# Attention statistics and their first rows issued from ScalarE's queue, and computed earlier

## The chip, the cores and the metric

The program runs on one core of one Trainium2 chip. The metric is the device time of one execution in microseconds (us). A core has a matrix engine (PE, TensorE), a vector engine (DVE), a scalar engine (ACT, ScalarE), a general one (POOL, GpSimd) and a synchronisation engine (SP), each with an instruction stream of its own that it works off in order. In this program DMA transfers are issued from SP's stream, apart from a few at the start which are issued from ACT's.

## The reference

Eight images of 768 channels and 32 x 32 positions (1024 tokens), in fp32, pass two layers; each adds to its input what it computes from the group-normalised input.

```python
# layer 0: attention in which scores are an outer product of variances
q, k, v = qkv of gn(x), 12 heads of 64 channels
var_v = var(v, over the head's channels); var_k = var(k, likewise)
attn = softmax(var_v @ var_k.T * 64**-0.5); x = x + proj(attn @ v) + b
# layer 1: 1x1 convolution over the features and 28 local correlations
f = gn(x); fn = f / max(norm(f), 1e-12)
corr = [sum(shift(fn, r, c) * fn) for 28 offsets (r, c) of a 7 x 7 window]
x = x + conv1x1(concat(f, corr)) + b
```

The queries are not used. A score is a product of one number per query token (the variance of its value vector) and one per key token, so an exponential is computed by ScalarE from a row of `var_v`, broadcast over 128 partitions, with a scale per partition from `var_k`.

## The kernel before

Channels or tokens lie on the 128 partitions. Large products are made by a scheme with seven block products in place of eight (`PAIR`, `SINGLE`); product p = 1 comes first in its PSUM bank, and 6, 7 and 4 are added to the same bank after the vector engine has read what stood there (`Banks`, line 316; `BANK`, line 59).

**The stages of an image b.** `KeysValues` (line 506) multiplies the normalised image with the key and value weights in two halves of six heads (`half` 0 and 1), one unit of `KV_US` = 1.94 us after another, and takes head statistics of the results on DVE (`kbn`, `vbn`). After the last unit of a half, `spread` (line 601) makes variances of them on DVE (`head_m2`), and a maximum over the partitions on POOL (`most`). `values` turns the value variances with a PE transpose (`ptv`), copies them on DVE (`rsv`) and stores them in DRAM as rows (`vdr`): this is `to_rows`, line 498. `keys` makes `nk`, the scales of the exponentials, on DVE; `rows` stores them the same way (`ptk`, `rsk`, `kdr`), only where a pair of that half needs them.

`Attention` (line 826) works on six pairs of heads (`Pair`, hp = 0 to 5; 0 to 2 belong to half 0, 3 to 5 to half 1). Per pair, `Pair.rows` (line 660) loads for each head the row of `vdr` broadcast over 128 partitions (`bc`, 512 KB). Eight steps t follow. A step is two exponentials on ACT (`ex`, 128 x 1024, line 674) and eight products on PE (`av`, line 699); at most three steps of exponentials stand ahead of PE (`AHEAD`). PE runs four steps at a time (`STEPS`). The softmax denominators come in one of two ways. For pairs in `SUMMED` (3, 4, 5; in image 0 also 0) DVE adds the exponentials (`acc`), and PE sums over partitions. For the others ACT makes a second set of exponentials over rows of `kdr` (`bk`, also 512 KB) and keeps only their sums (`junk`, line 684). The inverse sums go through DRAM (`it`, `ir`, `di`) and come back broadcast (`rd`, line 771), and DVE multiplies them into the pair's result (`v<-v,rd`).

Then `project` (line 1185) makes the output projection, adds it to the image (`f`), stores it (`x1d`) and normalises it. `Corr` (line 997) makes products of f with itself (`gr`) and from them the correlations (`win`, `dd`, `dn`, the transpose `ct`, `cs`), and `Conv` (line 1090) the convolution of layer 1, in units of the class `Wide` (line 914), loading `x1d` back as its accumulator.

**What overlaps.** Half 1 of image b, the correlations and the convolution of image b - 1 run on PE between the attention steps of image b (`work_off`, line 1168). Half 0 of an image is worked off ahead of its attention. In image 0 half 0 of image 1 stands in the convolution's place.

**What sets the order.** There is no scheduler on the chip. The program is written by Python code with a clock of estimates (`Clock`, line 71): `later.after(us, job)` places a job that many microseconds on in the planned time, `later.after_dve(us, job)` counted from the time at which DVE is planned to be free. A job emits its instructions when its time comes, so these figures fix the order on every engine, not the time at which anything runs. `ready` is a set of names that other parts of the plan wait for; `rows_at` and `rd_at` are the planned arrivals of `bc`, `bk` and `rd`; `Banks.product` plans the reading of a bank. What an instruction really waits for is given by semaphores. Transfers of one queue are issued in the order in which the plan emits them; eight semaphores are used by all of them in turn.

Of the kernel before, what the change touches and what calls it, by code (L numbers as in the profile page):

```python
# [13 lines left out]
P = 128  # L14
NB, C, H, W = 8, 768, 32, 32
N = H * W
J = C // P
NH, HD = 12, 64
HP = NH // 2
MT = N // P  # L20
HF = N // 2
# [27 lines left out]
KV_US, T_US, CORR_US = 1.94, 2.6, 1.05  # L49
# [16 lines left out]
def windows(ap, *dims):  # L66

    return bass.AP(tensor=ap.tensor, offset=ap.offset, ap=[list(d) for d in dims])
# [83 lines left out]
def two_layers(ctx, tc, x, wkv, wproj, bproj, wconv, wcorr, bconv, out):  # L152
    nc = tc.nc
# [28 lines left out]
    clock = Clock()  # L182
    later = clock
    vector = Vector(nc.vector, clock)
    ready = set()
# [40 lines left out]
    class WeightSums:  # L226


        def __init__(self, which, *queues):
            self.which = which  # L230
            flat = image_tile(fpool, "f", f"ws{which}").rearrange("p j n -> p (j n)")
            self.at = [flat[:, n * JH * KW : (n + 1) * JH * KW] for n in range(5)]
            for n in range(4):
                r, c = divmod(n, 2)
                queue = queues[n % len(queues)]
                if which in (0, 1):
                    queue.dma_start(out=self.at[n].rearrange("p (k m) -> p k m", k=JH), in_=kv_block(which, r, c))
                else:
                    to = self.at[n].rearrange("p (k m) -> p k m", k=JH)
                    queue.dma_start(out=to, in_=t_block(which, r, c).rearrange("p k i m -> p k (i m)"))  # L240
# [111 lines left out]
    banks = Banks()  # L352
# [9 lines left out]
    for base, sign in ((0, 1), (3, -1)):  # L362
        nc.gpsimd.affine_select(
            out=group, in_=group, compare_op=ALU.is_ge, fill=0.0, base=base,
# [133 lines left out]
    def to_rows(cols, dr, name):  # L498

        pt = small(f"pt{name}")  # L500
        nc.tensor.transpose(pt[0 : MT * HH, 0:P], cols.rearrange("p h t -> p (h t)"), ident)
        rs = work([MT * HH, P], f"rs{name}")
        vector.tensor_copy(rs, pt[0 : MT * HH, 0:P])
        nc.sync.dma_start(out=dr.rearrange("h (t p) -> (h t) p", p=P), in_=rs)

    class KeysValues:

# [46 lines left out]
        def unit(self, half, d, n, g, p):  # L554
            b = self.b
            if n == 0:
                self.make_sums(half, (2 * d, 2 * d + 1))
            s = self.sums[g]
            a = {1: self.block(g, 0, 0), 2: self.block(g, 0, 1), 4: self.block(g, 1, 1)}
            a.update({5: s[:, 0], 6: s[:, 1], 7: s[:, 2], 3: s[:, 3]})  # L560
            w = kv_stream.tiles[b, half, d, p]
            pairs = [(a[p][:, k, :], w[:, k, :]) for k in range(JH)]
            banks.product(g, p, KV_US, KW, pairs, lambda ps: self.take(half, g, p, ps))
            if p not in [q for _, q in PAIR[n + 1 :]]:
                kv_stream.done((b, half, d, p))
            if d == 1 and n == len(PAIR) - 1:
                self.over = half == 1
                later.after(KV_US + 0.5, lambda: later.after_dve(0.0, lambda: self.spread(half)))

        def stats(self, kind, half, t, src):  # L570
            if (kind, half) not in self.bn:
# [36 lines left out]
        def spread(self, half):  # L608
            b = self.b
            name = f"{b}_{half}"  # L610
            km2 = st.tile([P, HH, MT], F32, tag="km2", bufs=2, name=f"km2{name}")
            head_m2(self.bn["k", half], km2, f"k{name}")
            top = st.tile([P, HH], F32, tag="top", name=f"top{name}")
            vector.tensor_reduce(top, km2, AX.X, ALU.max)
            most = st.tile([P, HH], F32, tag="most", name=f"most{name}")
            nc.gpsimd.partition_all_reduce(most, top, P, bass_isa.ReduceOp.max)
            m2 = st.tile([P, HH, MT], F32, tag="vm2", bufs=4, name=f"vm2{name}")
            head_m2(self.bn["v", half], m2, f"v{name}")
            nk = st.tile([P, HH, MT], F32, tag="nk", bufs=4, name=f"nk{name}")
            kdr, vdr = [dpool.tile([HH, N], F32, tag=f"{kind}dr", name=f"{kind}dr{name}") for kind in "kv"]  # L620
            for of, new in ((self.m2, m2), (self.nk, nk), (self.kdr, kdr), (self.vdr, vdr)):
                of.append(new)

            def values():
                to_rows(m2, vdr, f"v{name}")
                ready.add(("v", b, half))

            def keys():
                for h in range(HH):
                    vector.tensor_scalar(  # L630
                        nk[:, h, :], km2[:, h, :], most[:, h : h + 1], HD ** -0.5 / (HD - 1) ** 2,
                        ALU.subtract, ALU.mult,
                    )
                ready.add(("nk", b, half))
                if not set(SUMMED[b > 0]).issuperset(range(3 * half, 3 * half + 3)):
                    later.after_dve(0.5, rows)

            def rows():
                to_rows(nk, kdr, f"k{name}")
                ready.add(("k", b, half))  # L640

            later.after_dve(2.5, values)
            later.after_dve(3.5, keys)


    class Pair:
# [13 lines left out]
        def rows(self, kind, e):  # L660

            pl, of = (bcpool, self.kv.vdr) if kind == "c" else (bkpool, self.kv.kdr)
            h = self.heads()[e][1]
            bc = pl.tile([P, N], F32, tag=f"b{kind}", name=f"b{kind}{self.b}_{self.hp}_{e}")
            nc.sync.dma_start(out=bc, in_=windows(of[self.half][h : h + 1, :], (0, P), (1, N)))
            (self.bc if kind == "c" else self.bk).append(bc)
            self.rows_at[kind, e] = clock.now + (9.0 if self.hp % (HP // 2) == 0 else 6.0)

        def exponentials(self, t):

# [95 lines left out]
        def load_inverses(self, rows):  # L766
            if self.before and not self.before.finished:
                return later.after(0.5, lambda: self.load_inverses(rows))
            self.rd = rdpool.tile([P, N], F32, tag="rd", name=f"rd{self.b}_{self.hp}")
            for e in range(2):  # L770
                nc.sync.dma_start(out=self.rd[e * HD : (e + 1) * HD, :], in_=windows(rows[e], (0, HD), (1, N)))
            self.rd_at = clock.now + 6.0
            self.try_finish()

        def sum_up_last(self):
# [136 lines left out]


    class Wide:
        def __init__(self, kind, name, acc, bias, operand, finished, more=None):
            self.kind, self.name, self.acc, self.bias = kind, name, acc, bias
            self.operand, self.finished, self.more, self.held = operand, finished, more, []

        def unit(self, g, p):
            w = t_stream.take(self.kind, g, p)  # L920
            pairs = [(w[:, k, :], self.operand(p, k)) for k in range(JH)]
            taken = lambda ps: self.take(g, p, ps)
            more = self.more(g, p) if self.more else None
            if more is None:
                banks.product(g, p, T_US, HF, pairs, taken)
            else:
                self.held.append((*banks.begin(g, p, HF, pairs, stop=False), taken, *more))
                if len(self.held) == 2:
                    self.join()
            t_stream.fill()  # L930
# [159 lines left out]
    class Conv:  # L1090
# [8 lines left out]
        def start(self):  # L1099
            if self.acc is None:  # L1100
                self.acc = image_tile(xnpool, "xn", f"x1_{self.b}")
                for n, us in ((0, 0.0), (1, 1.0), (3, 2.5), (4, 4.0), (2, 12.0), (5, 14.0)):
                    later.after(us, lambda n=n: nc.sync.dma_start(out=self.acc[:, n, :], in_=x1_dram[self.b][:, n, :]))
            if self.b == NB - 1:
                self.sums.third = [expool.tile([P, N], F32, tag="ex", name=f"t3_{k}")[:, :HF] for k in range(JH)]
            later.after(3.5, self.sums.second)
            self.wide = Wide(
                "c", f"c{self.b}", self.acc, bconv_sb, self.sums.operand, lambda i, hf: self.done(i, hf, "f"), self.more
            )
            ready.add(("acc", self.b))  # L1110
            later.after(7.0, self.thirds)
# [73 lines left out]
    def project(b, ots):  # L1185
# [16 lines left out]
        def normalise():  # L1202
            norm = Norm(bn, f"b{b}")
            later.after_dve(0.3, norm.means)
            later.after_dve(3.0, norm.spreads)

            def apply():
                to = f if b + 1 < NB else image_tile(xnpool, "xn", "f_last")
                layer1.append((to, f))
                norm.apply(to, f, ("f", b), 2.0 if b + 1 < NB else 0.0)  # L1210

            later.after_dve(5.0, apply)

# [4 lines left out]
        late = True  # L1218
        for n, (us, _, unit) in enumerate(wide.units()):
            if n == 4:  # L1220
                clock.wait(("ot", b, HP - 1), ready=ready)
            if late and n > 1 and ("ot", b, HP - 1) in ready:
                late = False
# [138 lines left out]
```

## Time and profile before

| | |
|---|---|
| median of 3 runs | 2762.36 us (2757.72 to 2765.87) |
| the profiled execution, its own time | 2773.49 us |
| its span, first to last instruction | 2771.8 us |
| mean granted TensorE clock | 0.993 |
| PE busy | 2712.3 us (98%) |
| DVE busy | 1664.1 us (60%) |
| ACT busy | 1362.3 us (49%) |
| DMA engines, mean traffic | 163 GB/s |

How lines of the profile are read. In a window's line stand the window, its length, and for PE, PEld (weight loads), DVE, ACT and POOL the busy time with the number of instructions, then the granted PE clock (1.00 is full), the busy share of the 16 DMA engines and GB/s. A waits line names engine, result and line, what it waited for, the sum in us, how often, and the longest. The chain followed back from the end of a window gives start, duration and what; "SPq" is SP issuing a transfer, "DMA a<-b" the time of that transfer as far as it was waited for. Names come without their numbers. Matmuls overlap in the record, so an engine can be busy throughout a window and yet do less in it than in another; the count of instructions shows that.

### The profile page before, as it was taken

How to read it: one execution, taken by the hardware profiler on the slowest of the kernel's cores; microseconds unless marked ns; L12 is line 12 of the kernel's file. 1: busy time of each engine (PE TensorE's matmuls, PEld its weight loads, DVE VectorE, ACT ScalarE, POOL GpSimd, SP SyncE). 2: the span in 40 equal slices, each digit the busy share in tenths (PEclk: the TensorE clock that was granted, in tenths of full speed). 3: DMA queues.
4: the chain of work that ended last, by engine and by line, in shares of the span. 5: the costliest groups of instructions: out<-in, count | busy, mean ns of one | idle time of the engine just before them, and what ended most of it. 6: DMA issues, size and time to landing. Idle time of an engine off the chain costs nothing.

```text
span 2771.8 us, 28821 instructions
## 1 busy us (share of the span) xinstructions
PE 2712.3 (98%) x9063; PEld 1277.7 (46%) x9063; DVE 1664.1 (60%) x4163; ACT 1362.3 (49%) x1814; POOL 307.0 (11%) x350
## 2 busy tenths in 40 slices
PE   6999999999999999999999999999999999999999
PEld 3543454335643455434554346533465334653353
DVE  4858734685447854478534884358743587446853
ACT  1398078520596106970079701886019850298400
POOL 3420101002200031000310012100121001110000
PEclk9999999999999999999999999999999999999999
DMA  8764454545554545536456365563654536535323
GB/s 302 280 227 150 142 189 122 163 165 160 175 150 143 187 154 157 165 128 204 150 158 189 97 203 168 149 181 91 228 175 130 182 97 222 171 113 170 117 73 95
DMA packets 324579, 451.85 MB, mean 163 GB/s; under 512 B 59794, under 2 KB 245890, under 8 KB 324426
## 3 DMA queue, kind: packets, MB, share of 16 engines
q1 hardware_dynamic: 322618, 444.88, 50.8%
q10 hardware_dynamic: 1808, 5.11, 0.5%
q8 instruction: 73, 1.20, 0.2%
q14 instruction: 80, 0.66, 0.1%
HBM read 380.44 MB, written 67.38 MB: 162 GB/s over the span
## 4 chain that ended last, share of the span: by engine, by line
PE 74%; issue 10%; DMA 5%; ACT 5%; DVE 4%; SPq 1%; POOL 1%; DVEq 0%; POOLq 0%; ACTq 0%
PE x L342 29%; PE av L699 17%; PE y L342 14%; PE z L342 8%; ACT ex L674 3%; PE gr L1006 2%; DMA rd<-di 2%; ACT junk L684 2%; DMA bc<-vdr 1%; DVE dn L146 1%; PE den L732 1%; PE z L936 1%; PE x L936 1%; PE den L782 1%; DVE cs L146 0%
## 5 line engine op out<-in xcount | busy, mean ns | idle before, releaser
L674 ACT ACTIVATE ex<-bc,nk 128x1024 f32<-128x1024 f32 x768 | 834.5, 1138 | 493.6 <-DMA bc<-vdr 271.3
L699 PE MATMUL av<-ex,v 128*64 128x512 f32 x3072 | 709.1, 601 | 12.3 <-ACT ex L674 12.3
L684 ACT ACTIVATE junk<-bk,vm 128x1024 bf16<-128x1024 f32 x368 | 420.5, 1143 | 41.9 <-DMA bk<-kdr 35.6
L699 PEld LDWEIGHTS av<-ex,v 128*64 128x64 f32 x3072 | 218.7, 138 | 473.9 <-issue 394.4
L146 DVE TENSOR_TENSOR acc<-acc,ex 128x1024 f32<-128x1024 f32 x350 | 401.6, 1212 | 0.0
L209 ACT COPY kp<-x 128x384 f32<-128x384 f32 x28 | 13.3, 479 | 558.1 <-PE x L342 558.1
L342 PE MATMUL y<-kv,s 128*128 128x384 f32 x768 | 267.8, 489 | 2.6 <-DMA kv<-kvs 2.6
L342 PE MATMUL x<-kv,xn 128*128 128x384 f32 x768 | 263.9, 490 | 4.4 <-DVE xn L146 3.3
L342 PE MATMUL x<-kv,s 128*128 128x384 f32 x768 | 262.2, 489 | 3.3 <-POOL s L546 3.3
L342 PEld LDWEIGHTS x<-kv,xn 128*128 128x128 f32 x768 | 145.1, 191 | 108.6 <-issue 14.3
L342 PEld LDWEIGHTS x<-kv,s 128*128 128x128 f32 x768 | 145.4, 191 | 104.1 <-issue 6.8
L342 PEld LDWEIGHTS y<-kv,s 128*128 128x128 f32 x768 | 142.4, 190 | 102.1 <-issue 8.7
L1006 PE MATMUL gr<-f 128*128 128x227 f32 (+1 forms) x672 | 131.8, 346 | 0.0
L342 PE MATMUL z<-kv,xn 128*128 128x384 f32 x384 | 130.1, 488 | 0.0
L342 PE MATMUL x<-v,wt 128*128 128x512 f32 x288 | 130.0, 596 | 0.0
L1006 PEld LDWEIGHTS gr<-f 128*128 128x128 f32 x672 | 121.2, 190 | 18.7 <-issue 6.2
L146 DVE TENSOR_TENSOR v<-y,v 128x128 f32<-128x128 f32 x180 | 40.9, 282 | 136.5 <-PE y L342 136.5
L342 PE MATMUL x<-f,wt 128*128 128x512 f32 x252 | 115.4, 598 | 0.1
L452 POOL TENSOR_TENSOR rstda<-vea,neghalf 128x1 f32<-128x1 f32 x8 | 4.8, 597 | 930.2 <-DVE vea L146 930.2
L546 POOL TENSOR_TENSOR s<-xn 128x384 f32<-128x384 f32 x64 | 68.5, 1080 | 309.6 <-PE x L342 219.4
L146 DVE BATCH_NORM_STATS2 vbn<-v 128x6 f32<-128x64 f32 x720 | 101.7, 210 | 0.0
L146 DVE COPY acc<-ex 128x1024 f32<-128x1024 f32 x50 | 33.7, 703 | 107.6 <-ACT junk L684 36.8
(170 smaller groups left out, 2925.0 us busy)
## 6 DMA issues: line engine op xcount, KB each, us to landing
kv<-kvs SPq DMA_DIRECT2D x128, 576.0 KB
kv<-in_wkv_dram SPq DMA_DIRECT2D x96, 576.0 KB
bc<-vdr SPq DMA_DIRECT2D x96, 512.0 KB
f<-in_x_dram SPq DMA_DIRECT2D x48, 512.0 KB
bk<-kdr SPq DMA_DIRECT2D x46, 512.0 KB
x1d<-f SPq DMA_DIRECT2D x42, 512.0 KB
x<-x1d SPq DMA_DIRECT2D x42, 512.0 KB
out_dram<-x SPq DMA_DIRECT2D x84, 256.0 KB
```

What stands on the lines that cost most here:

```text
L146: return getattr(self.engine, name)(*args, **kw)
L209: nc.scalar.copy(to, at)
L342: nc.tensor.matmul(t, lhsT=lhsT, rhs=rhs, start=p in FIRST and k == 0, stop=stop and k == len(pairs) - 1, skip_group_check=True,)
L452: nc.gpsimd.tensor_tensor(self.rstd, ve, neghalf[:, 0:1], ALU.pow)
L546: nc.gpsimd.tensor_tensor(self.sums[g][:, 0], a[g][2], a[g][3], ALU.add)
L674: nc.scalar.activation(ex, self.bc[e], AF.Exp, scale=self.kv.nk[self.half][:, h, t : t + 1])
L684: nc.scalar.activation(junk, self.bk[e], AF.Exp, scale=self.kv.m2[self.half][:, h, t : t + 1], accum_out=self.sums[:, e, t : t + 1],)
L699: nc.tensor.matmul(self.av[e * HD : (e + 1) * HD, hf, :], lhsT=self.vt[:, t, e, :], rhs=exs[e][:, hf * HF : (hf + 1) * HF], start=t == 0, ...
L732: nc.tensor.matmul(den[at * 32 : (at + 1) * 32, :], lhsT=ones[:, 0:32], rhs=self.acc[e][:, hf * HF : (hf + 1) * HF], start=True, stop=True,)
L782: nc.tensor.matmul(den[e * HD : (e + 1) * HD, :], lhsT=ones, rhs=self.acc[e][:, at], start=True, stop=True)
L936: nc.tensor.matmul(t, lhsT=wcorr_sb[at, i, :], rhs=cs[at, tokens, :], start=False, stop=True, skip_group_check=True)
L1006: nc.tensor.matmul(ps[:, :n], lhsT=f[:, j, t * P : (t + 1) * P], rhs=f[:, j, t * P : t * P + n], start=j == 0, stop=j == J - 1,)
```

## The change

Seven edits:

- `to_rows` issues its store (vdr, kdr) from ACT's queue instead of SP's.
- `Pair.rows` issues the loads of bc and bk from ACT's queue for the first pair of each half (hp = 0 and 3); the others stay on SP's. The planned arrival for these is 7.0 us on instead of 9.0.
- `spread` is planned 0.3 us after the last unit and emitted at once; before it was 0.5 us and then when DVE is planned to be free.
- `values` and `keys` follow at 1.0 and 2.2 us in images from 1 on (2.5 and 3.5 before and, still, in image 0). The rows count as ready 3.0 us after DVE's copy instead of at once.
- `rd_at` is 9.0 us on instead of 6.0 for pairs 0 to 3 in images from 1 on.
- `Wide` gets a flag, `loading`. Where the convolution's accumulator is being loaded, the banks of p = 1 of its first two column blocks are read 4.0 us later in the plan.
- In the projection of image 0 the slices of the normalisation are planned 1.0 us apart instead of 2.0.

```diff
@@ to_rows
-        nc.sync.dma_start(out=dr.rearrange("h (t p) -> (h t) p", p=P), in_=rs)
+        nc.scalar.dma_start(out=dr.rearrange("h (t p) -> (h t) p", p=P), in_=rs)
@@ KeysValues.unit
-                later.after(KV_US + 0.5, lambda: later.after_dve(0.0, lambda: self.spread(half)))
+                later.after(KV_US + 0.3, lambda: self.spread(half))
@@ KeysValues.spread
             def values():
                 to_rows(m2, vdr, f"v{name}")
-                ready.add(("v", b, half))
+                later.after_dve(3.0, lambda: ready.add(("v", b, half)))
...
             def rows():
                 to_rows(nk, kdr, f"k{name}")
-                ready.add(("k", b, half))
-
-            later.after_dve(2.5, values)
-            later.after_dve(3.5, keys)
+                later.after_dve(3.0, lambda: ready.add(("k", b, half)))
+
+            later.after_dve(1.0 if b else 2.5, values)
+            later.after_dve(2.2 if b else 3.5, keys)
@@ Pair.rows
-            nc.sync.dma_start(out=bc, in_=windows(of[self.half][h : h + 1, :], (0, P), (1, N)))
+            queue = nc.scalar if self.hp % (HP // 2) == 0 else nc.sync
+            queue.dma_start(out=bc, in_=windows(of[self.half][h : h + 1, :], (0, P), (1, N)))
             (self.bc if kind == "c" else self.bk).append(bc)
-            self.rows_at[kind, e] = clock.now + (9.0 if self.hp % (HP // 2) == 0 else 6.0)
+            self.rows_at[kind, e] = clock.now + (7.0 if self.hp % (HP // 2) == 0 else 6.0)
@@ Pair.load_inverses
-            self.rd_at = clock.now + 6.0
+            self.rd_at = clock.now + (9.0 if self.b and self.hp < HP - 2 else 6.0)
@@ Wide.unit
-                banks.product(g, p, T_US, HF, pairs, taken)
+                late = 4.0 if p == 1 and g < 2 and self.loading else 0.0
+                banks.product(g, p, T_US + late, HF, pairs, taken)
@@ Conv.start
             self.wide = Wide(
-                "c", f"c{self.b}", self.acc, bconv_sb, self.sums.operand, lambda i, hf: self.done(i, hf, "f"), self.more
+                "c", f"c{self.b}", self.acc, bconv_sb, self.sums.operand, lambda i, hf: self.done(i, hf, "f"), self.more,
+                loading=self.b < NB - 1,
             )
@@ project, apply
-                norm.apply(to, f, ("f", b), 2.0 if b + 1 < NB else 0.0)
+                norm.apply(to, f, ("f", b), (1.0 if b == 0 else 2.0) if b + 1 < NB else 0.0)
```

More of the change, by code (lines that the diff above doesn't have):

```diff
@@ L914, in two_layers, with __init__ @@
     class Wide:
-        def __init__(self, kind, name, acc, bias, operand, finished, more=None):
+        def __init__(self, kind, name, acc, bias, operand, finished, more=None, loading=False):
+            self.loading = loading
             self.kind, self.name, self.acc, self.bias = kind, name, acc, bias
```

## The prediction

> **What bounds the kernel now.** I read the page's busy row first, then TensorE's waits by stretch of the program, then the same kind of place in each image, then the chain.
>
> ```profile
> PE 2712.3 (98%) x9063; PEld 1277.7 (46%) x9063; DVE 1664.1 (60%) x4163; ACT 1362.3 (49%) x1814; POOL 307.0 (11%) x350
> ```
>
> TensorE is the bound. The change removes no product, so all it can win is time in which TensorE waits or is paced. Its waits in 300 to 580 us (image 1) and 580 to 2600 us (images 2 to 7):
>
> ```profile
> PE av L699 <- ACT ex L674: 6.6, 2, 5.0
> PE ct L1052 <- DVE dn L146: 3.1, 1, 3.1
> PE x L342 <- DVE t2o L146: 1.6, 1, 1.6
> ...
> PE av L699 <- ACT ex L674: 4.5, 11, 1.5
> PE ct L1052 <- DVE dn L146: 2.1, 6, 0.5
> PE ptv L501 <- DVE vm L146: 1.8, 5, 0.5
> ```
>
> These sums look too small to matter, but they hide pacing. Windows of 12 us at the first pair of the second half (hp = 3) in images 2, 3 and 7, and in image 1 at that pair and at `ct`:
>
> ```profile
> 836.00:848.00 12.00, 10.99 (x35) 3.46 (x34) 1.35 (x2) 7.38 (x7) 0.00 (x0) 1.00 0.93 287
> 1175.00:1187.00 12.00, 10.11 (x28) 3.04 (x28) 2.23 (x4) 6.69 (x7) 0.00 (x0) 0.86 0.91 304
> 2527.00:2539.00 12.00, 12.00 (x44) 3.86 (x42) 4.22 (x6) 9.97 (x11) 0.00 (x0) 1.00 0.78 247
> 505.00:517.00 12.00, 6.96 (x17) 2.01 (x14) 8.63 (x9) 6.71 (x7) 0.00 (x0) 0.73 0.42 117
> 417.00:429.00 12.00, 8.89 (x30) 4.11 (x31) 7.75 (x9) 8.57 (x13) 7.54 (x8) 0.72 0.24 67
> ```
>
> Busy shares hardly differ; the counts (28 to 44 products) do. Thirty-two `av` products take 7.02 us when fed; from start to start this group took 10.51 (with 1.12 in front) at 841.7, 10.5 (1.87) at 1181.4, 10.6 at 1519, 10.5 (0.6) at 1858, 8.81 at 2195 and 8.27 at 2531: 4.6 + 5.4 + 3.6 + 4.1 + 1.8 + 1.25 = 20.7 us lost. Image 1 loses 3.45 at its first pair (367), 3.1 + 2.7 at `ct` (422.7) and 8.8 at 501 to 518. The chain in image 3 says why:
>
> ```profile
> 1158.18 12.26 DMA rd<-di
> ...
> 1170.53 1.10 DVE v L146
> ...
> 1171.67 0.28 DVE rsv L146
> 1171.98 1.45 DMA vdr<-rsv
> 1173.44 0.32 SPq L665
> ...
> 1173.81 7.56 DMA bc<-vdr
> ```
>
> The transpose `ptv` ran at 1161.4, but its copy `rsv` stood on DVE behind x<-x1d loads and behind `rd`: ten microseconds. Then vdr, the broadcasts and ScalarE's exponentials follow, just in time or late. At image 1:
>
> ```profile
> 495.86 7.60 DMA di<-ir
> ...
> 504.07 4.20 DMA rd<-di
> ...
> 510.30 1.16 ACT ex L674
> ```
>
> **The Trainium skill.** "DMA: Bandwidth & Descriptors", Issuing engines are not separate DMA queues: moving a DMA to another engine saves only sequencer time, the 16 engines are shared. The trace agrees that issuing is cheap (SP 0.32 to 0.43 us) beside 5 to 7 us from issue to landing of a broadcast. The same page, Queues, rings and completion order: each DMA engine takes turns between rows that have work. SP and ACT have a row each, so a broadcast on ACT's need not stand behind SP's backlog; before has no such pair to show it. "Perfetto Trace Analysis", DMA Instruction — HWDGE: the semaphore wait happens on the issuing sequencer. The trace agrees: SP's vdr issue stood from 1161.6 to 1172.0 for `rsv`. So on ScalarE such an issue holds exponentials. "TensorE: Matmul & The Clock Gate", What's actually happening: half clock after about 3.4 us of idling. Here already a 1.6 us wait at 1181 goes with a granted 0.86[...].
>
> **The change, part by part.** No instruction is added or removed; 9 issues an image (two vdr, one kdr, four bc, two bk) move from SP to ACT. At SP's 0.4 us that is 3.6 us an image of an engine busy 49%: nothing in itself, but where it stands before an exponential it counts in full, and it is counted so below. The planner's new figures (7.0 for a first pair's rows, 9.0 for `rd`, the read of the product p = 1 taken 4.0 us later, 3.0 until rows count as ready, 1.0 between the slices of image 0's normalisation) issue nothing and act through the order alone; the orders used below hold all of them.
>
> *Second half, images 2 to 7.* Let E be the end of the last key product (1145.58 + 3.87 = 1149.5 in image 3). Before: rsv E+22.2, bc issued E+24, ex E+30.7, `av` E+31.9 and then paced by ScalarE. In the new order DVE does the spread right behind the last statistics (E+1.5 to 3.2), then t2f (3 x 0.7) and rsv, all ahead of the x1d take. PE: one conv unit (2.58), three steps (3 x 1.76), so ptv at E+8.0; rsv E+8.3; ScalarE reaches vdr about a microsecond earlier and waits it out. vdr to bc 1.4 us, but the issue stands behind two copies of the previous pair's result: E+13. Landing 5 to 7 us later lies beside six `junk` (6 x 1.2 = 7.3 us). First ex at E+20.5 to 22.5. PE reaches that pair after the step, six conv units (6 x 2.58) and a transpose: E+25.7, 4.3 us earlier than before, as two units now lie behind it. A step of exponentials takes 2.1 us against PE's 1.76, so it is late only past E+23. I take 0.6 us left of a mean 3.45: -2.85 each, -17 for six. Bounds: nothing left (-21), all left (0).
>
> What is late next: x<-t2f on PE (about E+20) needs a bank that DVE empties behind `v*rd`. `rd` is now issued ahead of the x1d loads, near E+4; with the 12.3 us it took, E+16, plus 1.1 + 2.1 + 1.4 us on DVE: E+20.6. No cost taken, 3 us at worst.
>
> *First half, images 2 to 7.* The broadcasts go out 0.9 us later, behind kdr, side by side with SP's bc of the next pair (1 MB more in flight); bk right behind the first exponential instead of at 1058.1. In image 3 bk landed at 1065.0, and step 3 of the first pair had 0.2 us to spare. The pair starts a unit (1.94 us) earlier on PE. bk lands 1063.5 to 1065, so I take a wait of 0.75 us: +4.5 for six (bounds 0 and +12).
>
> *Image 1.* First pair: SP stood from 340.9 to 351.7 for weight buffers, and bc went out at 354 to 357; through ACT it goes at about 320 to 330: -3.45. `ct` is placed behind four more steps (7 us), so its 3.1 + 2.7 becomes about 0.6: -5.2. Second half: `di` and `rd` no longer stand behind a weight load (rd issued 503.5, landed 508.3); estimated landing E+22 to 24 (E = 476.3), limit E+25: -8.8, or 0 if it is later. Sum -17.
>
> *Image 0.* vdr stands between exponentials of pair 2 and waits for rsv (about 170.6, ScalarE is there at 169.5); the bc issues behind it share semaphores with small loads that SP is still issuing. Pair 2 (173.7) had -1.0 us of slack in its last step: +1.5. In the projection the order on DVE is now takes, rsv, nk, v*acc, t2o. Before, x<-t2o waited 1.6 us for this:
>
> ```profile
> 305.11 1.10 DVE v L146
> 306.21 0.61 DVE t2o L146
> ```
>
> The last take ends near 305.9, plus 0.3 + 0.6 + 1.2 + 0.6 = 308.6, where PE is ready at 305.4: 3.2 us, 1.6 more, and about 1.5 of low clock: +3. Together +4.5 (0 to +8).
>
> Sum: -17 + 4.5 - 17 + 4.5 = -25, and with a few tenths from waits of ptv (1.8 us before) -26. Against the profiled execution, 2773.49 us (span 2771.8 and 1.7 around it), that is 2747.5; that execution lies 11 us above the median, and my figure is 2762.4 - 26 = 2736.
>
> **The rivals.**
>
> *The wait only moves* (0.17). `rd` or x1d lands late beside SP's and ACT's broadcasts, and x<-t2f waits 3 us in each of six images: +18, total -8, 2754. For it: rd took 12.3 us, and the estimate above has no room. Against it: rd's place on SP is ahead of what it stood behind.
>
> *Nothing comes through* (0.07): the stalls vary by image (1.25 to 5.4 us), so they may be given back elsewhere while TensorE at 98% sets the pace; 2762. Against it: the order on PE differs after these places only by what is said above.
>
> *ScalarE's queue blocks* (0.12), the slower side. One place: the vdr and bc issues stand in order between exponentials, and 1 us of their wait is 1 us for everything behind. If rsv (held by an x1d take, 4.6 us before) or the landing of vdr and bk is 4 us later than I have it, the second half keeps its loss and gains 2 us (6 x (2.85 + 2) = +29), the first half has 2 us more (+12): 2736 + 41 = 2777. It decides from about 4 us of loss per image (26 us over six and a half images). For it: slack of 0.2 us in the first half. Against it: rsv is now ahead of that take.
>
> **How the numbers follow.** The likeliest case has 0.64 and a range of its own of 2722 to 2750. Two measurements of this kernel can be told apart from about 0.3% (8.3 us), so faster means below 2754, slower above 2770.7. Faster: 0.63 of the likeliest and half of the moved wait, 0.09, together 0.72. Slower: the blocked queue and an edge, 0.13. Same: the rest, 0.15. The range from 2722 to 2764 leaves out the blocked queue (0.12), and about 0.06 below.
>
> **What would show it.** Right: rsv some 9 us after the last key product in the second half, no releaser bc of `ex` there, over 42 products in the 12 us windows of images 2 to 6; TensorE's wait for `dn` in image 1 below 1 us; t2o's wait in image 0 grown to 3. Wrong: ScalarE idle for vdr or bk over 3 us in most images, `av` waits for `ex` in step 3 of the first pair above 2 us, or new waits of x<-t2f. What would make the number wrong without that is landing time: the 5 to 7 us for a broadcast with two rows in flight is not shown before.

## The result and the profile after

The changed kernel takes 2770.9 us (median of 15 runs, 2764.86 to 2776.42), the kernel before 2763.6 us (15 runs, 2754.66 to 2770.31). The ratio is 1.003, 95% interval 1.0018 to 1.0042: slower by 0.3%, where 2736 us and a gain of about 1% were forecast. The profiled execution of the changed kernel spans 2769.2 us and lies on its median.

The busy row of the page hides it, as before:

```profile
PE 2706.1 (98%) x9063; PEld 1275.6 (46%) x9063; DVE 1661.3 (60%) x4163; ACT 1355.2 (49%) x1814; POOL 303.9 (11%) x350
```

TensorE's waits of the changed kernel, in 300 to 580 us and then in 580 to 2600 us (engine, result and line, what it waited for; sum, times, longest):

```profile
PE x L342 <- DVE x L146: 4.1, 2, 2.4
PE x L342 <- DVE t2o L146: 3.5, 1, 3.5
PE av L700 <- ACT ex L675: 0.6, 1, 0.6
...
PE av L700 <- ACT ex L675: 6.6, 6, 1.7
PE x L342 <- DVE x L146: 6.6, 4, 2.1
PE ct L1055 <- DVE dn L146: 1.4, 4, 0.5
```

What was forecast to go is gone: no 5 us wait at pair 3 of image 1, no 3 us at `ct`. Two rows are new or larger: `av` waits once in each of images 2 to 7, now at the first pair of the first half and longer, and in images 3 to 6 a product of the convolution waits for DVE's reading of its bank (`x`).

Windows of 12 us in the second half, pair 3, of images 2, 3 and 7, to be set beside those of before:

```profile
836.00:848.00 12.00, 12.00 (x50) 4.00 (x48) 11.72 (x12) 9.28 (x10) 0.00 (x0) 1.00 0.60 184
1172.00:1184.00 12.00, 12.00 (x48) 3.90 (x48) 11.25 (x13) 8.96 (x9) 0.00 (x0) 1.00 0.50 135
2527.00:2539.00 12.00, 12.00 (x48) 3.94 (x50) 11.72 (x13) 10.82 (x11) 0.00 (x0) 1.00 0.37 96
```

48 to 50 products instead of 28 to 44: the stall that the change aimed at is cured in these images. The chain through the second half of image 3 shows what replaced it:

```profile
1153.09 0.24 PE ptv L501
...
1153.35 0.29 DVE rsv L146
...
1153.67 3.85 DMA vdr<-rsv
1157.52 0.02 issue
1157.53 0.33 SPq L1106
1157.86 0.04 issue
1157.90 7.44 DMA x<-x1d
...
1165.44 1.42 DVE x L146 x2
...
1166.91 2.84 PE x L342 x6
```

The copy `rsv` now follows its transpose at once. But an x1d load on SP starts only when vdr, on ACT's queue, has landed, and everything below hangs on that load. SP's waits in 1145 to 1165 us say it directly:

```profile
SPq L1106 <- DMA vdr<-rsv: 6.4, 1, 6.4
...
SPq L1106 <- DMA bc<-vdr: 3.3, 1, 3.3
```

The data of x1d have nothing to do with vdr. In the built program the completion semaphores (the counters that tell that a transfer has landed) are given to the transfers of SP and ACT in one common turn of eight; in the trace they have the numbers 100 to 105, 107 and 108. In image 3 the vdr store and the second x1d load both have number 102, and the load waits for 102 alone, that is until vdr's count is complete.

SP stands so in every image from 2 on, but it costs time only where the x1d loads come too late for it. In image 2 they are held for 5.4 us, vdr lands 1.6 us after its issue, and no product waits; in image 7 the hold falls on a weight load (L306) behind the four x1d loads, and no product waits either. The two lines, image 2 and image 7:

```profile
SPq L1106 <- DMA vdr<-rsv: 5.4, 1, 5.4
...
SPq L306 <- DMA vdr<-rsv: 6.4, 1, 6.4
```

And the chain through the first half of image 3:

```profile
1039.91 0.11 PE ptv L501
...
1042.83 0.38 ACTq L666
1043.22 0.04 issue
1043.26 9.15 DMA bc<-vdr
...
1052.52 6.50 DMA bk<-kdr
```

The pair's second broadcast of 512 KB took 9.15 us; the exponential on the first one started at 1050.7, 7.8 us after its issue at 1042.8. In the kernel before, the first two broadcasts were issued at 1049.0 and 1049.35, and the first exponential started at 1054.1: 5 us.

```profile
L665 SPq DMA_DIRECT2D bc<-vdr x4: 319/376/430, 1049.0 to 1050.3; - x4
L674 ACT ACTIVATE ex<-bc,nk x4: 1132/1140/1148, 1054.1 to 1057.5; 128x1024 f32<-128x1024 f32 x4
```

The chain goes on: bk is issued from ScalarE's stream right behind that second exponential and lands at 1059.0. ScalarE waits for it, and TensorE, after three of the pair's first four steps, for ScalarE (1050 to 1068 us):

```profile
ACT junk L685 <- DMA bk<-kdr: 1.2, 1, 1.2
...
PE av L700 <- ACT ex L675: 1.6, 1, 1.6
```

**The balance.** For each group of like products on PE (32 of `av`, 12 of a projection unit and so on) I take the time from its start to the next group's, less what such a group takes undisturbed; the sum of the surplus and a constant 2663 us gives the span of every kernel here within 1 us (before 2771.8 - 108.9, after 2769.2 - 106.1). In the table `x<-t2f` is the convolution unit at which the wait for x1d appears; `t2o`, further down, is the operand of a projection unit in image 0. The profiled execution of before had run 10 us over its median, so it was profiled again (b_again below, span 2760.3). Surplus in us:

| place | before | before again | after | forecast of the difference |
|---|---|---|---|---|
| images 2 to 7, second half, first pair | 20.1 | 15.5 | 0.0 | -17 |
| images 2 to 7, x<-t2f | 1.1 | 1.2 | 9.8 | 0 |
| images 2 to 7, first half, first pair | 0.9 | 1.0 | 16.9 | +4.5 |
| image 1, attention and what runs between | 19.5 | 19.5 | 9.6 | -17 |
| image 0 | 16.0 | 15.2 | 21.9 | +4.5 |
| start and tail | 30.3 | 23.4 | 27.6 | 0 |
| all other | 21.0 | 21.3 | 20.3 | 0 |
| sum | 108.9 | 97.1 | 106.1 | -25 |

Against the second profile the sum rises by 9.0 us; the medians differ by 7.3. The start and the tail, which no edit touches, differ by 6.9 us between the two profiles of the same kernel, so the 4.2 us there are no effect of the change that these profiles can show.

### The profile page after: what moved, and what is told of

Same layout as the page of the kernel before. It is cut to its first block, busy times and chain, and to the rows that moved or that the text cites. A ratio compares the mean times of both kernels' runs of the same rounds, so it can differ in the third digit from the quotient of the medians.

```text
span 2769.2 us, 28860 instructions
## 1 busy us (share of the span) xinstructions
PE 2706.1 (98%) x9063; PEld 1275.6 (46%) x9063; DVE 1661.3 (60%) x4163; ACT 1355.2 (49%) x1814; POOL 303.9 (11%) x350
## 4 chain that ended last, share of the span: by engine, by line
PE 83%; issue 8%; DMA 5%; DVE 3%; ACT 0%; POOL 0%; SPq 0%; ACTq 0%; DVEq 0%; POOLq 0%
PE x L342 32%; PE av L700 21%; PE y L342 15%; PE z L342 9%; PE gr L1009 3%; DMA x<-x1d 1%; DMA vdr<-rsv 1%; DMA bc<-vdr 1%; DVE dn L146 1%; PE den L733 1%; PE z L939 1%; PE x L939 1%; PE den L783 1%; PE y L939 1%; DMA rd<-di 0%
## 5 line engine op out<-in xcount | busy, mean ns | idle before, releaser
L700 PE MATMUL av<-ex,v 128*64 128x512 f32 x3072 | 698.9, 596 | 9.4 <-ACT ex L675 9.0
L146 DVE TENSOR_TENSOR v<-x,v 128x128 f32<-128x128 f32 x180 | 41.0, 282 | 91.9 <-PE x L342 91.7
```

The lines of the kernel that those rows point to most:

```text
L146: return getattr(self.engine, name)(*args, **kw)
L700: nc.tensor.matmul(self.av[e * HD : (e + 1) * HD, hf, :], lhsT=self.vt[:, t, e, :], rhs=exs[e][:, hf * HF : (hf + 1) * HF], start=t == 0, ...
```

## The experiments

PE's and DVE's orders are planned without regard to queues, so a transfer can be moved between queues and the two orders stay as they are, instruction for instruction. That gives a clean table of two by two: old or new placement, old or new queues.

**New placement, old queues (a_all_sp).**

```diff
-        nc.scalar.dma_start(out=dr.rearrange("h (t p) -> (h t) p", p=P), in_=rs)
+        nc.sync.dma_start(out=dr.rearrange("h (t p) -> (h t) p", p=P), in_=rs)
-            queue = nc.scalar if self.hp % (HP // 2) == 0 else nc.sync
+            queue = nc.sync
```

> The changed kernel with all its transfers issued from SP again; the orders on PE and DVE are those of the changed kernel. Theory 1 (two new waits made by ScalarE's queue: the first broadcasts of the first half land late, 2.8 us in each of images 2 to 7, and SP's x1d loads stand for vdr, 2.3 us in images 2 to 6): both waits go or fall under 1 us, A3 stays cured, 20 to 27 us less than the changed kernel, ratio to before 0.993 to 0.996. Theory 2 (the new order on DVE and PE is itself the cause): the waits stay, ratio near 1.003.

2742.8 us, ratio 0.9928 (0.9916 to 0.9941): 28 us less than the changed kernel, a little more than the 20 to 27 expected. Of images 2 to 7 nothing is left: first pairs 0.4 and 0.0 us, x<-t2f 0.5. TensorE's waits in 580 to 2600 us have one row left:

```profile
PE ct L1055 <- DVE dn L146: 0.6, 3, 0.2
```

SP's waits in 1140 to 1160 us of it:

```profile
SPq L1088 <- DVE kp L146: 4.5, 1, 4.5
...
SPq L666 <- DMA vdr<-rsv: 2.4, 1, 2.4
SPq L504 <- DVE rsv L146: 0.6, 1, 0.6
```

On SP the vdr store stands behind the first four x1d loads, waits 0.6 us for `rsv`, and none of the four waits for it. TensorE, DVE and ScalarE run the same instructions in the same order in both kernels. So the placement is worth -20 us, and theory 2 falls.

**Old placement, new queues (b_act).**

```diff
-        nc.sync.dma_start(out=dr.rearrange("h (t p) -> (h t) p", p=P), in_=rs)
+        nc.scalar.dma_start(out=dr.rearrange("h (t p) -> (h t) p", p=P), in_=rs)
-            nc.sync.dma_start(out=bc, in_=windows(of[self.half][h : h + 1, :], (0, P), (1, N)))
+            (nc.scalar if self.hp % (HP // 2) == 0 else nc.sync).dma_start(out=bc, in_=windows(...))
```

> The kernel before with only the queue edits (vdr, kdr, and the first pairs' bc and bk on ACT); PE and DVE orders as before. Theory 1: the stall at the first pair of the second half stays (rsv is as late as before), x1d is issued ahead of vdr and so not held, the first half has a unit more of room; ratio 0.999 to 1.003. Theory 2: ratio 1.000. A gain of more than 0.4% would say that the queue was worth something on its own.

2803.1 us, ratio 1.0153 (1.0138 to 1.0167): a clear miss of what theory 1 expected. The queue costs 40 us in the old placement and 28 in the new (2770.9 against 2742.8). ScalarE's waits in 1160 to 1180 us, image 3's second half:

```profile
ACT junk L684 <- DVE nk L146: 8.0, 1, 8.0
ACT junk L684 <- DMA vdr<-rsv: 0.9, 1, 0.9
```

ScalarE stands 8.0 us at the vdr store (the releaser is named by the DVE instruction after `rsv`) and 0.9 at the broadcasts, with eight `junk` behind it, so the first exponential of pair 3 comes 20.1 us after ptv, against 18.8 and 15.7 in the two profiles of before. The surplus at these pairs is 38.9 us instead of 15.5. In the first half ScalarE's order puts kdr behind the first exponentials, which themselves wait for `bc`: kdr goes out 12.0 us after ptv (before: 4.6), and bk after that; surplus 17.9 instead of 1.0.

**Which of the two queue edits (b_store_act, b_rows_act).** The two halves of that diff alone, on the kernel before.

> The kernel before with only vdr and kdr stored from ACT. Theory: in the second half the vdr issue waits on ACT in front of eight junk for rsv, so the first exponential of pair 3 comes some 2 to 3 us later, about 3 us lost in each of images 2 to 7; in the first half nothing, as bk is issued late anyway; ratio 1.004 to 1.008. If stores do not matter there, 1.000.

2789.7 us, ratio 1.0097 (1.0077 to 1.0118). The mechanism is as expected, the size above it: first exponential of pair 3 at 19.6 us after ptv, surplus at these pairs 34.0. ScalarE's wait in 1158 to 1183 us:

```profile
ACT junk L684 <- DVE nk L146: 8.6, 1, 8.6
```

> The kernel before with only the first pairs' bc and bk loaded from ACT. Theory: beside SP's broadcasts of the next pair these take 7 to 9 us instead of 5 in either half; the second half, which is on the edge, loses 1 to 2 us more, the first half up to 1; ratio 1.003 to 1.008. If two queues do not share evenly, 1.000.

2791.1 us, ratio 1.0105 (1.0084 to 1.0126). The sign was right and the reason wrong. The landing of the broadcasts is not what is late in the second half; ScalarE stands 8.9 us at the issue of `bc`, waiting for vdr to land, and the same eight `junk` behind it move the exponential to 19.8 us after ptv. In the first half the first exponential came at 9.5 us after ptv (before 7.1), so two queues do share, but it cost nothing there (0.1 us), probably since the pair then still has the unit of room that the new placement takes away; that was not tried by itself. In 1160 to 1185 us:

```profile
ACT junk L684 <- DMA vdr<-rsv: 8.9, 1, 8.9
```

**The first half: crowding or a slow queue (a_rows0_sp, a_bc1_late).** The first sends the urgent broadcasts down SP's queue, ahead of the next pair's; the second leaves them on ACT and holds the next pair's back.

```diff
-            queue = nc.scalar if self.hp % (HP // 2) == 0 else nc.sync
+            queue = nc.scalar if self.hp == HP // 2 else nc.sync
```

> The changed kernel with bc and bk of the first half's first pair on SP, those of the second half and all stores on ACT. Theory 1: the first exponential of the first half comes about 3 us earlier, the wait of 2.3 to 3.1 us at that pair in images 2 to 7 goes (-14 to -17 us), x<-t2f stays; ratio to before 0.997 to 0.999. Rival (the DMA engines are simply full there, whichever queue issues): the waits stay, 1.003.

2759.2 us, ratio 0.9983 (0.9975 to 0.9991). First exponential 8.0 us after ptv instead of 10.9, surplus at these pairs 0.5 instead of 16.9; x<-t2f stays (11.3). Image 1's first pair loses what it had gained, since SP is blocked there again (5.0 us).

```diff
-                    if ("c", e) not in pair.rows_at and (hp < 2 or ...passes["e"] == MT):
+                    if ("c", e) not in pair.rows_at and (hp < 2 or ...passes["e"] == MT) and (hp != 1 or self.made):
```

> The changed kernel with one edit: the broadcasts of the second pair (hp = 1, on SP) are issued only after the first exponential of the first pair has been planned; queues as in the change. Theory 1 in its sharper form (a broadcast on ACT's queue and one on SP's share the DMA engines evenly, so the urgent pair takes 8 to 9 us instead of 5): first exponential of the first half some 8 us after ptv instead of 11, the wait of 2.3 to 3.1 us gone, 13 to 17 us less than the changed kernel, ratio to before 0.997 to 0.999. Rival (ACT's queue itself is slow, or kdr ahead of the broadcasts holds them): exponential still near 11, ratio 1.003.

2754.5 us, ratio 0.9965 (0.9953 to 0.9976), a little better than expected. Instructions on `bc` in the first half of image 3, first of the changed kernel, then of this one (first and last start at the end):

```profile
L666 SPq DMA_DIRECT2D bc<-vdr x2: 372/391/410, 1041.9 to 1042.4; - x2
L666 ACTq DMA_DIRECT2D bc<-vdr x2: 382/500/617, 1042.8 to 1043.3; - x2
L675 ACT ACTIVATE ex<-bc,nk x2: 1148/1148/1148, 1050.7 to 1052.5; 128x1024 f32<-128x1024 f32 x2
```

```profile
L675 ACT ACTIVATE ex<-bc,nk x5: 1133/1134/1152, 1042.7 to 1047.5; 128x1024 f32<-128x1024 f32 x5
L666 ACTq DMA_DIRECT2D bc<-vdr x2: 383/412/442, 1038.3 to 1038.7; - x2
L666 SPq DMA_DIRECT2D bc<-vdr x2: 465/468/472, 1042.7 to 1043.2; - x2
```

From the issue on ACT to the exponential 7.8 us with SP's two broadcasts in flight, 4.4 us without. ACT's queue is not slow, nor does kdr ahead of it hold it; two pairs of broadcasts on two queues move side by side, and the urgent one ends nearly when both end. In one queue the first came first (4.8 us in a_all_sp with four in it). Both runs agree, and the rivals fall.

**x<-t2f: the common semaphore or the traffic (a_vdr_pool).** Only the second half's vdr store, from image 1 on, goes out from POOL, whose transfers have semaphores of their own (number 113 in the trace).

```diff
-        nc.scalar.dma_start(out=dr.rearrange("h (t p) -> (h t) p", p=P), in_=rs)
+        (nc.gpsimd if name[0] == "v" and name[-1] == "1" and name[1] != "0" else nc.scalar).dma_start(...)
```

> The changed kernel with only the second half's vdr store issued from POOL from image 1 on, so that no SP transfer shares a completion semaphore with it; orders on PE, DVE and SP unchanged. Theory 1: SP issues x1d without the gap of 6.4 us (1151.1 to 1157.5 in image 3), x<-t2f waits under 0.5 us in images 2 to 6, 8 to 12 us less than the changed kernel, ratio 0.998 to 1.000. Rival (x1d is late because rd and the broadcasts fill the DMA engines): the gap goes but x1d lands as late, x<-t2f waits as before, 1.003.

2764.7 us, ratio 1.0008 (0.9999 to 1.0017). SP's waits in 1145 to 1166 us:

```profile
SPq L306 <- DMA bc<-vdr: 10.9, 1, 10.9
SPq L1088 <- DVE kp L146: 4.5, 1, 4.5
SPq L1106 <- DMA rd<-di: 1.1, 2, 0.8
```

TensorE's waits in 580 to 2600 us:

```profile
PE av L700 <- ACT ex L675: 4.6, 6, 1.4
PE ct L1055 <- DVE dn L146: 0.9, 4, 0.3
```

The wait of an x1d load for vdr is gone, and x<-t2f with it: 0.5 us of surplus instead of 9.8. The gain is 6.2 us where 8 to 12 were expected, because 2.6 us came back at pair 3: from POOL vdr took 6.2 us to land in image 3, from ACT 3.85. SP now stands 10.9 us for a broadcast of ACT's, the next collision of the same kind, but behind it are only weights that nobody needs yet. Image 7 of the changed kernel is the counter-test: SP stands for vdr as long, but with no x1d load, and x<-t2f does not wait.

**Both cures together (a_both).** The edits of a_bc1_late and a_vdr_pool.

> The changed kernel with both cures at once, its queues kept otherwise: the second pair's broadcasts wait for the first exponential, and the second half's vdr goes out from POOL. If the two waits are all that the queue costs, the gains add (-16.3 and -6.1 us of the changed kernel's 2770.9): near 2748, ratio 0.993 to 0.9955, level with a_all_sp. If a third cost of ACT's queue is left: 0.996 or more.

2747.1 us, ratio 0.9949 (0.9935 to 0.9963), as expected. In images 2 to 7 2.3 us are left at the first half's first pair, 1.9 at the second half's, 0.5 at x<-t2f. The two waits are nearly all that ACT's queue costs there.

**The spread's place alone (b_spread).** The kernel before with the edits of `unit` and `spread`, and neither the queue nor the other figures.

> The kernel before with only the placement of spread, values and keys and the 3.0 us until rows count as ready; queues and the other figures as before. If the spread's place alone cures the second half: first exponential of pair 3 some 8 us earlier, ratio 0.993 to 0.996. If the later reading of the convolution's banks and rd's later time are needed with it: rsv still stands behind other work or x<-t2f waits, 0.997 to 1.002.

2754.0 us, ratio 0.9972 (0.9962 to 0.9982): the second alternative. The stall at pair 3 falls from 15.5 to 10.9 us only. In image 3 `rsv` stands 6.4 us behind ptv (7.8 in the second profile of before, 0.3 in a_all_sp), because on DVE the convolution's first banks are read in front of it and wait for x1d; DVE's waits in 1146 to 1160 us:

```profile
DVE x L146 <- DMA x<-x1d: 6.2, 2, 3.2
```

So the later reading of the banks, or one of the other figures that came with it, is needed for the cure; which of them was not separated.

**The kernel before once more (b_again).**

> The kernel before, profiled once more, because its profiled execution took 10 us more than its median while that of the changed kernel lay on its median. If the surplus was in the stalls that the forecast took as gains: span near 2761, with less than 49 us in the sum of those of images 1 to 7. If the surplus lies elsewhere: the same stalls within 3 us.

2762.6 us, ratio 0.9998 (0.9989 to 1.0007), span 2760.3. Between the two alternatives: 4.6 us of the 11.8 us of surplus that the first profile has over the second lie in the stalls of the second half, 6.9 at the start and the tail, which no edit touches. Image 1's stalls are the same in both (19.5). In image 3 the 12 us window at pair 3 has 40 products at full clock, where the first profile had 28 at 0.86:

```profile
1169.00:1181.00 12.00, 12.00 (x40) 4.73 (x38) 1.92 (x4) 8.08 (x9) 0.00 (x0) 1.00 0.92 291
```

**A version that beats both (c_two).** a_all_sp, but image 1's first-half stores and first rows on ACT, and the spread of that half placed as in the kernel before.

```diff
-        nc.sync.dma_start(out=dr.rearrange("h (t p) -> (h t) p", p=P), in_=rs)
+        (nc.scalar if name[1:] == "1_0" else nc.sync).dma_start(...)
-            queue = nc.sync
+            queue = nc.scalar if self.b == 1 and self.hp == 0 else nc.sync
-                later.after(KV_US + 0.3, lambda: self.spread(half))
+                later.after(KV_US + 0.3, lambda: self.spread(half)) if (b, half) != (1, 0) else later.after(KV_US + 0.5, ...)
```

> All transfers on SP as in a_all_sp, but the stores and the first pair's rows of image 1's first half on ACT, and the spread of that half placed as in the kernel before. Theory: the 4.9 us at the first pair of image 1 and most of the 5.4 us at t2o in image 0 go, ratio to before 0.989 to 0.991 (a_all_sp had 0.9928). If SP was not what held image 1's rows, 0.992 to 0.993.

2734.3 us, ratio 0.9896 (0.9882 to 0.991), as expected. Image 1's first pair no longer waits (4.9 us in a_all_sp), and t2o is back at the 1.8 us of before (5.4). What is left in image 1 is the second half. TensorE's waits in 340 to 580 us:

```profile
PE av L700 <- ACT ex L675: 2.8, 1, 2.8
PE x L342 <- DVE x L146: 1.9, 1, 1.9
```

## Why the prediction was wrong

The forecast was -25 us of surplus, the second profile of before gives +9.0. Of the 34.0 us between them 11.4 are in the first half of images 2 to 7, 8.6 at x<-t2f, 7.1 in image 1, 4.2 at the start and the tail, 2.2 in image 0 and 1.5 in the second half; the rest is -1.0.

**The second half, images 2 to 7: right, its size by a profile that ran high.** Forecast -17 of 20.7; all of it went. `rsv` came 0.3 us behind ptv, exponentials at pair 3 wait for no broadcast. But a second profile of before shows 15.5 there, not 20. The prediction noted that its profiled execution lay 11 us above the median and then took that execution's stalls in full as gains against the median; some 5 us of them were not in the second profile.

**The first half: the mechanism right, the term mis-sized, and the largest miss.** "I take a wait of 0.75 us: +4.5 for six (bounds 0 and +12)"; measured 2.6 more each, +15.9, above the upper bound. The wait is where the prediction looked for it, in step 3 and for bk. It allowed 0.9 us for the later issue, and the issue was a microsecond later as said. It did not price the landing: 5.0 us before, 7.8 and 9.2 us with SP's broadcasts beside it, and bk goes out only behind the second exponential. The Trainium skill ("DMA: Bandwidth & Descriptors", Queues, rings and completion order: the DMA engines take turns between rows) was read as an advantage, not having to stand behind SP's backlog. SP had no backlog there; it had the next pair's broadcasts, which the old single queue served second. Taking turns also means that the urgent transfer shares the engines for as long as the other queue has work.

**"What is late next": a cost put at nothing.** It named the right place (x<-t2f waits for a bank that DVE empties), and put the danger at `rd`, with "No cost taken, 3 us at worst". rd landed in time: DVE multiplied it in at 1158.4 in image 3 without a wait. What was late was x1d, held on SP by vdr on ACT through a common semaphore: +8.6 us, 1.5 to 4.1 us in each of images 3 to 6 and nothing in 2 and 7. The prediction saw such coupling in image 0 only and did not ask, for each issue that moves, which later transfer on SP takes the same semaphore next. The rival "the wait only moves" had the place and named x1d beside rd, but with twice the size (18), and put its lateness down to the broadcasts instead of the semaphore.

**Image 1: two of three terms right.** First pair and `ct` gone as forecast (3.2 and 5.9 us in the second profile). Of the second half's -8.8 next to nothing came: pair 3 loses 1.9 us instead of 8.5, but x<-t2f and two units after it, ahead of that pair, now lose 6.4. The wait moved, as the prediction's "or 0 if it is later" allows. It estimated that rd lands 22 to 24 us after the last key product; rd landed 33.8 us after it (before: 32.0). It was issued 4.5 us earlier, counted from there, but took 10.53 us instead of 4.20:

```profile
478.36 6.03 DMA vdr<-rsv
...
489.33 4.21 DMA di<-ir
...
494.11 10.53 DMA rd<-di
```

SP stands 6.8 us for vdr there too, with a weight load, an x1d load and `di` behind it. That is not the whole cause: in a_all_sp, where nothing stands for vdr so, x<-t2f still loses 2.4 us and pair 3 4.5, and in a_vdr_pool 1.2 and 8.6. What else makes rd late here stays open. Net -9.9 instead of -17.

**Image 0: right in the main.** +4.5 forecast, +6.7 measured, within its bounds of 0 to +8. t2o's surplus grew from 1.8 to 5.4 us: 3.5 of it wait, as forecast 3.2, the rest low clock (granted 0.86 in 305 to 317 us). Pair 2 lost 1.0 instead of 1.5, and the very first pair 2.6, not forecast.

**The slower rival.** "ScalarE's queue blocks" was on the right side, but its test failed: in the changed kernel ScalarE is idle only 0.7 us for `rsv` in the second half of image 3. The blocking that it describes is real in the old placement, where b_act shows it at 8.0 us a half. In the new one the queue hurts SP and the DMA engines instead. That its "2 us more" in the first half lies near the measured miss (2.6 instead of 0.75) is in part luck: ScalarE stands there for late broadcasts, which the rival allowed for, but they were late because two queues shared the engines.

Added up against the second profile: -15.5 + 8.6 + 15.9 - 9.9 + 6.7 + 4.2 (start and tail) - 1.0 = +9.0 us.

## What to carry to other kernels

A transfer that is moved to another issuing engine is no longer ordered with its old neighbours, and that can work against an urgent transfer as well as for it: ask what it used to be ahead of, not only what it was behind. Where a program gives out completion semaphores in one turn to two queues, as this one does, read for every issue moved which semaphore it takes and which transfer of the other queue takes it next, for that one will stand until the moved one has landed; it costs only if something needed soon stands there, as in images 3 to 6. And before a stall of one profile is booked as a gain against a median, compare that execution's own time with the median; profile again if they differ.

## What the runs showed of the hardware

In the first half of image 3, two 512 KB broadcasts with no others in flight were usable from 4.4 us after issue (a_bc1_late); with two more of the same size issued on the other queue within a microsecond, after 7.8 us for the first and 9.2 us for the second (after), or 7.2 and 9.5 (b_act). Four on one queue kept the first at 4.8 us (a_all_sp) and 5.1 us (before). So the pair on ACT's queue had no precedence over the pair on SP's, and a fixed order in one queue was worth about 3 us to the first pair.

The store vdr (24 KB, to DRAM) took 1.45 us from issue to the next issue in image 3 of the kernel before. In the second halves of the changed kernel it took from 1.6 us (image 2) to 5.2 us (image 7), 3.85 us in image 3, where `rd` and x1d were in flight beside it. Its landing, not its issue, was what SP waited for.

An issue on ScalarE's queue that waits holds what stands behind it in ScalarE's stream: eight `junk` behind 8.0 us (b_act), 8.6 us (b_store_act) and 8.9 us (b_rows_act), and each of these kernels took 1.0 to 1.5% longer than before.

The length of a wait alone did not tell whether TensorE's clock falls: in one profile of before, a wait of 1.6 us goes with a granted 0.86 in the 12 us window at 1175 us and another of 1.6 us with 1.00 in the window at 305 us.
